# One merge over all units: projections two batches ahead, the network two units behind, maxima paced by VectorE

## The chip, the cores and the metric

The kernel runs on one core of one Trainium2 chip. The metric is the device time of one execution in microseconds, here the median of several runs. The engines of the core are TensorE (PE; its weight loads are shown as PEld), VectorE (DVE), ScalarE (ACT), GpSimd (POOL) and SyncE (SP), which issues the DMAs here. Each engine takes its instructions strictly in the order of its own queue, and waits on semaphores for the others.

## What is computed

The input x has 8 batches of 1024 tokens with 512 features, in float32. A layer norm without weights gives xn. The output is x plus causal attention of xn plus a gated network of xn, where the network's operands are first rounded to a 4-bit grid with one scale for each block of 16.

```python
def fp4_quant_dequant(x):
    xb = x.reshape(shape[:-1] + (shape[-1] // BLOCK, BLOCK))      # BLOCK = 16
    scale = jnp.maximum(jnp.max(jnp.abs(xb), axis=-1, keepdims=True) / 6.0, 1e-12)
    xn = xb / scale
    idx = jnp.searchsorted(_MID, jnp.abs(xn))
    return (_GRID[idx] * jnp.sign(xn) * scale).reshape(shape)

def fp4_linear(x, w):
    return jnp.einsum('bsk,nk->bsn', fp4_quant_dequant(x), fp4_quant_dequant(w))

# attention: 16 heads of 32, causal softmax, W_attn 512 x 1536, W_proj 512 x 512
qkv = xn @ W_attn + b_attn
att = softmax(where(causal, q @ k.T * 32 ** -0.5, -inf))
attn = (att @ v) @ W_proj + b_proj
# network: w_gate and w_up 1408 x 512, w_down 512 x 1408
ffn = fp4_linear(silu(fp4_linear(xn, w_gate)) * fp4_linear(xn, w_up), w_down)
out = x + attn + ffn
```

## The kernel before

**Tiles and units.** Tokens are cut into 64 tiles of 128 (eight to a batch, numbered n through all batches). Attention is cut into 64 units of two heads of one batch. So there are as many units as tiles, and the work of the kernel goes in steps of one unit and about one tile of everything else.

**The stages that a tile passes.** `load_tokens`, `normed` (layer norm on DVE, with a power on POOL) and `prepare` transpose a tile. After every second tile `project` makes q, k and v for the pair: six groups of 16 matmuls over W_attn pieces `wa`, loaded anew each time, two buffers deep. ACT evicts a group to `full` (one buffer; L443 for q and k, L486 for v), DVE splits q and k in a high and a low part for the fp32r matmuls (`high`, one buffer), and SP stores them to `qk_kept` in DRAM (L462), v to `v_kept`. The rounded tile `xq`, transposed, goes to `xq_kept` and comes back later as `xqT_in` for the network.

**The stages that a unit passes.** `load_half` and `load_values` bring q, k and v back from DRAM. `maxima` (L535 to L563) computes the scores once, 24 matmuls of up to 512 columns, and reduces each on DVE (L545) to the row maxima, which are transposed and sent through DRAM to `shT`. `weigh` subtracts them and computes the scores again in PSUM (L627 and L630), takes the exponential on ACT (L638), sums on POOL (L603), multiplies with v (L609), and stores `y` and the sums. `invert` makes their reciprocals.

**The network.** `network` goes through each tile in chunks of 512, 512 and 384 hidden columns: gate and up products (L768), silu on ACT, product and rounding on DVE (the class `Quantised`, L292 to L316), transposition (L323), down product into `acc` (L748). Its weights are rounded and transposed once by `weights_quantised`, in 34 pieces; the first `EARLY` pieces give two of their steps to POOL. `finish` loads `y` and the inverses of a tile (L840, L846), forms their product on DVE (L852, L853), does the output projection (L861), adds the network's part, and stores the result.

**What sets the order.** The order on every queue is fixed when the program is built, by a planner in the kernel. Each stage is a generator that yields (cost on PE, earliest time of its next step, number of PSUM banks that it needs). `merge` takes several such streams, keeps a planned clock, and advances the stream that has done the least share of its total, among those within `AHEAD_OF_OTHERS` of the last one; if no one can start, the planned clock moves. `Later` issues an action at a planned time. There are six banks, handed out by `Banks`. The costs that the planner assumes (`dve(0.65)`, `act(...)`) are written by hand.

**Before the change** there is one `merge` for each unit, over the streams weigh(n), maxima(n + 1), prepare and project of tile n + 10 (`AHEAD`), network of tile n - 8 (`LAG`) and finish of tile n - 10. It ends when every stream has ended. Ahead of unit 0 stand a merge of eight tiles' projections with 17 weight pieces, and one of two further tiles with the maxima of unit 0. In units 0 to 7, where no network can run yet, the other 17 weight pieces are rounded, and `prepare_late` reads x again, norms and rounds the tiles 0 to 7. Behind unit 63 come eight merges with one tile of network and one or two of finish each.

Of the kernel before, what the change touches and what calls it, by code (L numbers as in the profile page):

```python
# [19 lines left out]
P = 128  # L20
# [7 lines left out]
def kernel(  # L28
# [27 lines left out]

    nc = tc.nc
# [15 lines left out]
    AHEAD = 10  # L73
    LAG = 8
    SPREAD = 1.4
    HOP = 0.15
    TABLE = 1.3
    AHEAD_OF_OTHERS = 0.3
# [13 lines left out]
    dram = ctx.enter_context(tc.tile_pool(name="dram", bufs=4, space=DRAM))  # L92
# [48 lines left out]
    def act(columns, after=0.0, function="other"):  # L141
        if function == "other":
            function = table[0]
        switch = TABLE if function != table[0] else 0.0
        table[0] = function
        return on("act", 0.1 + 0.00095 * columns + switch, after)
# [31 lines left out]
    class Banks:  # L178
# [9 lines left out]
        def take(self):  # L188
            k = self.at.index(min(self.at))
            self.at[k] = float("inf")  # L190
            return k, self.tiles[k]
# [30 lines left out]
    def load_biases():  # L222
# [3 lines left out]
        wide = p1.tile([P, NC, P], F32, name="xqT")  # L226
# [16 lines left out]
    class Quantised:  # L243
# [38 lines left out]
        def operations(self, src, w, xs, helper):  # L282
# [6 lines left out]
            spreader, name, cost = (nc.gpsimd, "pool", 1.1) if helper else (nc.vector, "dve", 0.68)  # L289
# [6 lines left out]
            def powers():  # L296
# [7 lines left out]
                    0.65,  # L304
# [6 lines left out]
                (0.15, 0.55, "dve", scales),  # L311
                (cost, 0.0, name, lambda: spreader.tensor_tensor(blocks(xs), blocks(src), spread(inv), ALU.mult)),
                (0.9, 0.0, "dve", powers),
                (0.67, 0.0, "dve", lambda: nc.vector.tensor_tensor(xs, xs, step, ALU.add)),
                (0.67, 0.0, "dve", lambda: nc.vector.tensor_tensor(xs, xs, step, ALU.subtract)),
# [48 lines left out]
    def normed(tl):  # L364

        xt = tl.xt
        stats = p4.tile([P, 6], F32, name="stats")
        mv = p4.tile([P, 2], F32, name="mv")
        rstd = p4.tile([P, 1], F32, name="rstd")
        nc.vector.bn_stats(stats, xt)  # L370
        nc.vector.bn_aggr(mv, stats)
        nc.vector.tensor_scalar_add(rstd, mv[:, 1:2], EPS)
        nc.gpsimd.tensor_tensor(rstd, rstd, power, ALU.pow)
        yield 0.0, pool(0.6, dve(1.05)), 0
        nc.vector.tensor_scalar(xt, xt, mv[:, 0:1], rstd, ALU.subtract, ALU.mult)
        tl.ready = dve(0.6)
        if tl.n >= NT:
            tl.xs = Quantised(xt, D, p1.tile([P, CW], F32, name="xs"))

    def prepare(tl):  # L380
# [7 lines left out]
        if tl.n >= NT:  # L388
            yield from keep_quantised(tl, tl.xs)
# [7 lines left out]
    def prepare_late(tl):  # L397
        xt = p3.tile([P, D], F32, name="res")
        nc.sync.dma_start(out=xt, in_=x[tl.b, tl.t * P : (tl.t + 1) * P, :])
        tl.xt = xt  # L400
        yield 0.0, clock[0] + 4.0, 0
        yield from normed(tl)
        xq = Quantised(tl.xt, D, tl.xt, tl.ready)
        yield from keep_quantised(tl, xq)

    kept = []
# [6 lines left out]
    def keep_quantised(tl, xq):  # L413
        yield 0.0, xq.ready(), 1
        settle(kept)
        xqT = p1.tile([P, NC, P], F32, name="xqT")
        end = transposed(xqT, xq.done(), NC)
        tl.xq = dram.tile([P, NC, P], F32, name="xq_kept", bufs=AHEAD + LAG + 4)
        kept.append(Later(end - clock[0] + 0.5, lambda: nc.sync.dma_start(out=tl.xq, in_=xqT)))
        yield 0.45, 0.0, 0  # L420

    def project(batch, g, after):
        xnT = batch.xnT
        yield 0.0, after, 1
        for s in range(2):
            for f in range(0, NC, 2):
# [28 lines left out]
                def split(full=full, high=high, low=low):  # L455
                    nc.vector.tensor_copy(high, full)
                    nc.vector.tensor_tensor(low, full, high.bitcast(F32), ALU.subtract)
                    dve(1.1)
# [62 lines left out]
    def maxima(un):  # L521
# [4 lines left out]
        for t in range(NT):  # L526
            Q, i = t // QG, t % QG
            for r in range(HU):
                k = i * HU + r
                for h in range(Q + 1):  # L530
# [15 lines left out]
                    end = dve(0.08 + 0.00105 * n, end)  # L546
                    banks.back(bank, end)
                    yield cost, 0.0, 1
# [10 lines left out]
        yield 0.0, dve(1.1), 1, 0.3  # L559
# [23 lines left out]
    def weigh(un):  # L583
        f, r0 = un.u * HU // HPC, un.u * HU % HPC
        emptied = 0.0
        yield 0.0, un.ready, 2
        for Q in range(2):
# [5 lines left out]
            def summed(group):  # L593

                for r in range(HU):
# [4 lines left out]
                    else:  # L600
                        for pr, q0 in prs:
                            pool(0.1 + (W - q0) * 0.0024)
# [66 lines left out]
            added = free["pool"]  # L669
            yield 0.0, max(ready, emptied), 0  # L670
            yield weighted(), added, 1
# [16 lines left out]
            emptied = act(W)  # L688
            zs = p2.tile([P, W // 2], F32, name="zs")
            nc.scalar.copy(zs, z)  # L690
            end = act(W // 2, clock[0] + 0.65)
# [15 lines left out]
            yield 0.65, 0.0, 2  # L707


        def invert():  # L710
            flat = HU * S // P
            z = p2.tile([P, flat], F32, name="z")
            nc.sync.dma_start(out=z, in_=un.batch.sums[un.u].rearrange("q g (p e) -> (q g p) e", e=flat))
            inverses = un.batch.inverses[un.u].rearrange("q r (p e) -> (q r p) e", e=flat)
            Later(5.0, lambda: nc.vector.reciprocal(z, z))
            Later(8.0, lambda: nc.sync.dma_start(out=inverses, in_=z))


    def load(tl):
        tl.xqT = p3.tile([P, NC, P], F32, name="xqT_in")  # L720
        nc.sync.dma_start(out=tl.xqT, in_=tl.xq)
        tl.there = clock[0] + 4.0

    def network(tiles):
# [8 lines left out]
        def down(job):  # L733
# [12 lines left out]
            for j in range(job.w // P):  # L746
# [4 lines left out]
                if i == NI - 1:  # L751
# [4 lines left out]
                    tl.part = dram.tile([P, D], F32, name="part_kept", bufs=NT + 8)  # L756
# [6 lines left out]
        def product(job, wT):  # L763
            yield 0.0, job.tl.there, 1
# [19 lines left out]
        def hidden(job):  # L784
            nc.vector.tensor_tensor(job.hid, job.hid, job.g, ALU.mult)
            end = dve(0.65, max(job.gated, clock[0] + 1.72 * job.w / CW))
# [3 lines left out]
        def jobs():  # L790
            for tl, following in zip(tiles, tiles[1:] + [None]):
                if following is not None:
                    Later(4.0, lambda following=following: load(following))
# [33 lines left out]
    def finish(tl):  # L827
        t = tl.t

# [20 lines left out]
        part = load_part() if tl.part is not None else None  # L850
# [3 lines left out]
        yield 0.0, dve(1.4), 1, 1.0  # L854
        for half in range(2):
# [8 lines left out]
            if part is None:  # L864
                while tl.stored is None:
                    yield 0.0, clock[0] + 1.0, 0
                part = load_part()
                yield 0.0, clock[0] + 4.0, 0
            nc.vector.tensor_tensor(part[:, cols], po, part[:, cols], ALU.add)
            end = dve(0.42, clock[0] + 1.72)  # L870
            banks.back(k, end)
            yield 1.72, 0.0 if resident else clock[0] + 6.0, 1
        Later(end - clock[0] + 0.5, lambda: nc.sync.dma_start(out=out[tl.b, t * P : (t + 1) * P, :], in_=part))


    class Batch:
        def __init__(self):
# [4 lines left out]
            self.inverses = dram.tile([NU, 2, HU, W], F32, name="inv_kept")  # L882

# [4 lines left out]
    class Tile:  # L888
        def __init__(self, n):
            self.n, self.b, self.t = n, n // NT, n % NT  # L890
            self.part, self.stored, self.ready, self.there = None, None, 0.0, 0.0
# [6 lines left out]
    def merge(streams):  # L898

        live = [Stream(total, steps) for total, steps in ((t, s) for s, t in streams)]  # L900
        while live:
            least = min(s.share() for s in live)
            start = lambda s: max(s.ready, banks.when(s.banks))
            near = [s for s in live if s.share() - least < AHEAD_OF_OTHERS] or live
            now = [s for s in near if start(s) <= clock[0] + 0.05]
            if now:
                s = min(now, key=Stream.share)
# [9 lines left out]
    class Stream:  # L917
        def __init__(self, total, steps):
            self.total, self.steps = total, steps
            self.done, self.ready, self.banks = 0.0, 0.0, 0  # L920

        def share(self):
            return self.done / self.total

        def step(self):
            said = next(self.steps, None)
            if said is None:
                return False
            cost, self.ready, self.banks = said[:3]
            self.done += said[-1] if len(said) > 3 else cost  # L930
            passed(cost)
            return True

    def run(steps):
        merge([(steps, 1.0)])
# [21 lines left out]
    EARLY = PIECES // 2  # L957
    tiles = [Tile(n) for n in range(N)]
    units = [Unit(n) for n in range(N)]
    batches = []  # L960

# [7 lines left out]
    with tc.manual_schedule(  # L969
# [17 lines left out]
        head = itertools.chain(*[begin(n) for n in range(NT)])  # L987
        merge([(head, 10.7 * NT), (up_to(weights_steps, EARLY * 0.5, [0.0]), EARLY * 0.5)])
        for un in units:
            un.batch = None  # L990
        for n in range(3):
            units[n].batch = batches[0]
# [11 lines left out]
        merge([(itertools.chain(begin(NT), begin(NT + 1)), 22.0), (first_maxima(), 4.7)])  # L1004
        load_biases()
        late = [0.01]
        for n in range(N):
            if n == N - AHEAD + 1:
                for half in range(2):
                    wp = p2.tile([P, NC, 2 * P], F32, name="wa")  # L1010
                    nc.sync.dma_start(out=wp, in_=wp_in[:, :, half * 2 * P : (half + 1) * 2 * P])
                    resident.append(wp)
            streams = []
            while units[n].shT is None:
                passed(0.5)
            if n + 2 < N:
                units[n + 2].batch = batches[units[n + 2].b]

            def loads(n=n):
                if n + 1 < N:  # L1020
                    load_half(units[n + 1], 1)
                if n + 2 < N:
                    load_half(units[n + 2], 0)
                if n + 1 < N:
                    load_values(units[n + 1])

            Later(1.0, loads)
            if n + AHEAD < N:
# [62 lines left out]
```

## Time and profile before

| | us |
|---|---|
| three runs | 4860.23, 4861.45, 4874.52 |
| median | 4861.45 |
| the profiled execution, its own time | 4870.0 |
| the profiled execution, its span | 4868.3 |

| engine | busy us | share of the span | instructions |
|---|---|---|---|
| PE | 4445.5 | 91% | 18708 |
| PEld | 2643.2 | 54% | 18708 |
| DVE | 3326.0 | 68% | 6937 |
| ACT | 1459.5 | 30% | 2892 |
| POOL | 1847.5 | 38% | 2618 |

The mean granted clock of TensorE is 0.96. The span runs from the first to the last instruction. Busy times of matmuls overlap[...]. The profile's slices show the busy share of each engine in 40 equal parts of the span, in tenths; a line with L and a number names a line of the kernel, and an arrow "x <- y" in a list of waits says that x stood until y was done, with the total, the count and the longest one.

### The profile page before, as it was taken

What the parts mean: (1) busy time and instruction counts of PE and PEld (TensorE: products, weight loads), DVE (VectorE), ACT (ScalarE), POOL (GpSimd) and SP (SyncE); (2) the same over time, 40 slices, a digit from 0 to 9 for tenths busy, and PEclk for the clock granted to TensorE, in tenths of its full rate; (3) what the DMA queues carried; (4) which work ended last, traced back from release to release, by engine and by line L of the source; (5) the groups of instructions that cost most, each with busy time, mean ns of one, the idle gap of its engine ahead of it and who ended that gap; (6) DMA issues with size and microseconds to landing.
All of it is one profiled execution on the core that took longest, in us unless ns stands there. A gap on an engine that the chain in (4) does not pass through costs nothing.

```text
span 4868.3 us, 59460 instructions
## 1 busy us (share of the span) xinstructions
PE 4445.5 (91%) x18708; PEld 2643.2 (54%) x18708; DVE 3326.0 (68%) x6937; ACT 1459.5 (30%) x2892; POOL 1847.5 (38%) x2618
## 2 busy tenths in 40 slices
PE   6577779999999999999999999999999999999998
PEld 5444445555555555555555555555555555555544
DVE  5677776666776766667767676777766667766544
ACT  1122223333333333333333333333333333333200
POOL 2144444334343433443334334443333344444300
PEclk8778889999999999999999999999999999999999
DMA  5644443355444544554544455445444543332221
GB/s 173 179 111 119 112 119 103 106 148 145 127 138 136 140 121 137 148 142 124 140 137 136 123 150 142 133 133 141 136 121 136 146 133 103 84 90 75 68 63 54
DMA packets 609146, 605.36 MB, mean 124 GB/s; under 512 B 133824, under 2 KB 464064, under 8 KB 608832
## 3 DMA queue, kind: packets, MB, share of 16 engines
q1 hardware_dynamic: 608832, 601.57, 44.3%
q8 instruction: 149, 2.44, 0.2%
q14 instruction: 165, 1.35, 0.1%
HBM read 431.50 MB, written 169.87 MB: 124 GB/s over the span
## 4 chain that ended last, share of the span: by engine, by line
PE 53%; DVE 25%; DMA 11%; POOL 3%; SPq 3%; issue 2%; ACT 1%; ACTq 0%; DVEq 0%; POOLq 0%
PE bank L768 16%; PE acc L748 9%; DVE neg L545 4%; PE bank L432 4%; PE y L609 4%; PE bank L627 3%; PE bank L535 3%; PE bank L630 3%; PE bank L861 3%; PE bank L476 3%; DMA qs<-qk_kept 3%; PE bank L323 2%; DMA z<-sums_kept 2%; POOL sum L603 2%; DMA ks<-qk_kept 2%
## 5 line engine op out<-in xcount | busy, mean ns | idle before, releaser
L603 POOL TENSOR_TENSOR sum<-sum,pr 128x512 f32<-128x512 f32 (+3 forms) x1024 | 988.8, 976 | 749.3 <-ACT pr L638 714.2
L638 ACT ACTIVATE pr<-bank 128x512 f32<-128x512 f32 (+3 forms) x1536 | 679.5, 491 | 1070.2 <-PE bank L630 859.7
L545 DVE TENSOR_REDUCE neg<-bank 128x1 f32<-128x512 f32 (+3 forms) x1536 | 840.6, 555 | 173.6 <-PE bank L535 138.0
L543 DVE TENSOR_TENSOR bank<-bank,mask 128x128 f32<-128x128 f32 x1024 | 299.0, 292 | 655.6 <-PE bank L535 655.0
L535 PE MATMUL bank<-ks,qs 128*128 128x512 f32 (+3 forms) x1536 | 659.8, 472 | 85.8 <-DVE neg L545 46.1
L627 PE MATMUL bank<-shT,pick 128*128 128x512 f32 (+3 forms) x1536 | 653.4, 433 | 56.4 <-DVE neg L545 56.0
L768 PE MATMUL bank<-wgT,xqT_in 128*128 128x512 f32 (+1 forms) x1536 | 688.6, 578 | 3.8 <-ACT hqT L324 0.7
L768 PE MATMUL bank<-wuT,xqT_in 128*128 128x512 f32 (+1 forms) x1536 | 680.3, 574 | 2.2 <-ACT pr L638 2.1
L644 POOL TENSOR_SCALAR_AFFINE_SELECT pr<-pr 128x128 f32<-128x128 f32 x1024 | 344.8, 352 | 878.6 <-ACT pr L638 872.7
L748 PE MATMUL acc<-wdT,hqT 128*128 128x512 f32 x1408 | 670.7, 596 | 1.3 <-ACT hqT L324 1.3
L630 PE MATMUL bank<-qs,ks 128*128 128x512 f32 (+3 forms) x1536 | 531.4, 354 | 0.0
L598 POOL TENSOR_TENSOR sum<-pr 128x512 f32<-128x512 f32 x256 | 350.0, 1391 | 359.4 <-ACT pr L638 359.4
L432 PE MATMUL bank<-xnT,wa 128*128 128x256 f32 x2048 | 475.9, 387 | 3.2 <-DMA wa<-in_L_attn_W_attn_dram 1.4
L535 PEld LDWEIGHTS bank<-ks,qs 128*128 128x128 f32 x1536 | 281.6, 194 | 337.8 <-issue 123.7
L432 PEld LDWEIGHTS bank<-xnT,wa 128*128 128x128 f32 x2048 | 394.6, 195 | 81.4 <-issue 20.8
L609 PE MATMUL y<-pr,vs 128*32 128x512 f32 (+3 forms) x3072 | 391.2, 523 | 42.4 <-POOL pr L644 39.1
L627 PEld LDWEIGHTS bank<-shT,pick 128*128 128x128 f32 x1536 | 301.9, 197 | 228.0 <-DVE neg L545 90.1
L768 PEld LDWEIGHTS bank<-wgT,xqT_in 128*128 128x128 f32 x1536 | 273.2, 192 | 250.5 <-issue 191.8
L768 PEld LDWEIGHTS bank<-wuT,xqT_in 128*128 128x128 f32 x1536 | 285.0, 195 | 213.1 <-issue 160.6
L748 PEld LDWEIGHTS acc<-wdT,hqT 128*128 128x128 f32 x1408 | 255.5, 190 | 218.0 <-issue 202.4
L630 PEld LDWEIGHTS bank<-qs,ks 128*128 128x128 f32 x1536 | 301.7, 196 | 85.2 <-issue 52.0
L443 ACT ACTIVATE full<-bank,bqk 128x256 f32<-128x256 f32 x256 | 107.6, 472 | 630.5 <-PE bank L432 263.5
(98 smaller groups left out, 4833.5 us busy)
## 6 DMA issues: line engine op xcount, KB each, us to landing
wa<-in_L_attn_W_attn_dram SPq DMA_DIRECT2D x192, 512.0 KB
qs<-qk_kept SPq DMA_DIRECT2D x512, 128.0 KB
ks<-qk_kept SPq DMA_DIRECT2D x512, 128.0 KB
wp<-in_L_attn_W_proj_dram SPq DMA_DIRECT2D x93, 512.0 KB
qk_kept<-high SPq DMA_DIRECT2D x128, 256.0 KB
qk_kept<-full SPq DMA_DIRECT2D x128, 256.0 KB
y_kept<-yu SPq DMA_DIRECT2D x256, 128.0 KB
yT<-y_kept SPq DMA_DIRECT2D x128, 256.0 KB
```

Of the source, the lines that this page charges most:

```text
L432: nc.tensor.matmul(pq[:, j, :], lhsT=wa[:, c, j * P : (j + 1) * P], rhs=xnT[:, c, :], start=(c == 0), stop=(c == NC - 1),)
L535: nc.tensor.matmul(sc[:, :n], lhsT=un.qs[Q][:, r, i * P : (i + 1) * P], rhs=un.ks[h][:, r, :n], start=True, stop=True,)
L545: nc.vector.tensor_reduce(neg[:, Q + h, k : k + 1], sc[:, :n], AX.X, ALU.max, negate=True)
L598: nc.gpsimd.tensor_tensor(sums[r], prs[0][0], prs[1][0], ALU.add)
L603: nc.gpsimd.tensor_tensor(sums[r][:, q0:], sums[r][:, q0:], pr[:, q0:], ALU.add)
L609: nc.tensor.matmul(y[row : row + HD, q0:], lhsT=un.vs[h][:, jj, r * HD : (r + 1) * HD], rhs=pr[:, q0:], start=(j < 2), stop=(j >= last - 1 ...
L627: nc.tensor.matmul(w[:, q0:], lhsT=pick[:, Q * HU + r, :], rhs=un.shT[:, q0:], start=True, stop=False)
L630: nc.tensor.matmul(w[:, q0:], lhsT=un.ks[h][:, r, jj * P : (jj + 1) * P], rhs=un.qs[Q][:, r, q0:], start=False, stop=True,)
L638: nc.scalar.activation(pr[:, q0:], w[:, q0:], AF.Exp)
L644: nc.gpsimd.affine_select(out=pr[:, q0 : q0 + P], in_=pr[:, q0 : q0 + P], compare_op=ALU.is_ge, fill=0.0, base=0, pattern=[[1, P]], channe ...
L748: nc.tensor.matmul(tl.acc, lhsT=job.hqT[:, j, :], rhs=wdT[:, i, :], start=(i == 0), stop=(i == NI - 1))
L768: nc.tensor.matmul(job.g, lhsT=job.tl.xqT[:, c, :], rhs=wT[:, c, job.i0 : job.i0 + job.w], start=(c == 0), stop=(c == NC - 1),)
```

## The change

The merges of the single units give way to one merge over everything. A stream is now a row of parts; each part has a place on an axis that counts units (`begin`, `length`), and the merge advances the stream that is furthest back on this axis, among those within 0.6. Streams that could have started 0.4 us ago (`SURE`) go first.

- Projections run 16 tiles ahead of the units (formerly 10): the start projects two batches, in two merges, with 14 weight pieces beside each, and with the maxima of unit 0 in the second. Six pieces are left for the units 0 and 1.
- The network runs two units behind (formerly 8). `finish` of tile n begins at unit n + 10, once all units of its batch are done.
- `prepare_late` is gone. The normed tile is kept in DRAM (`xn_kept`), and `quantised` brings it back, rounds and transposes it one unit ahead of the network.
- `maxima` yields `free["dve"] - QUEUE` as the earliest time of its next step: DVE's planned queue has to be under 2 us. It begins 0.3 units earlier.
- The planner's costs are changed, mostly raised (DVE and POOL steps, `HOP` from 0.15 to 0.2); `finish` adds its halves by `Later`, and the reciprocals are planned 14 us after their load instead of 5.

The core of the diff:

```diff
-    AHEAD = 10
-    LAG = 8
+    AHEAD = 2 * NT
+    LAG = 2
+    LAST = NT + 2
+    SOONER = 0.3
+    QUEUE = 2.0
+    SURE = 0.4
...
-    HOP = 0.15
+    HOP = 0.2
     TABLE = 1.3
-    AHEAD_OF_OTHERS = 0.3
+    AHEAD_OF_OTHERS = 0.6
...
-            spreader, name, cost = (nc.gpsimd, "pool", 1.1) if helper else (nc.vector, "dve", 0.68)
+            spreader, name, cost = (nc.gpsimd, "pool", 1.35) if helper else (nc.vector, "dve", 0.7)
...
-                (0.9, 0.0, "dve", powers),
+                (1.14, 0.0, "dve", powers),
...
-        if tl.n >= NT:
-            tl.xs = Quantised(xt, D, p1.tile([P, CW], F32, name="xs"))
+        tl.xn = dram.tile([P, D], F32, name="xn_kept", bufs=AHEAD + LAG + 4)
+        tl.kept = Later(tl.ready - clock[0] + 0.5, lambda: nc.sync.dma_start(out=tl.xn, in_=xt))
...
+    def quantised(tl):
+
+        tl.kept.now()
+        xs = p1.tile([P, CW], F32, name="xs")
+        nc.sync.dma_start(out=xs, in_=tl.xn)
+        yield 0.0, clock[0] + 4.0, 0
+        xq = Quantised(xs, D, xs)
+        yield 0.0, xq.ready(), 1
+        xqT = p3.tile([P, NC, P], F32, name="xqT")
+        tl.there = transposed(xqT, xq.done(), NC)
+        tl.xqT = xqT
+        yield 0.45, 0.0, 0
...
-                    end = dve(0.08 + 0.00105 * n, end)
+                    end = dve(0.16 + 0.00103 * n, end)
                     banks.back(bank, end)
-                    yield cost, 0.0, 1
+                    yield cost, free["dve"] - QUEUE, 1
...
     def finish(tl):
         t = tl.t
+        while tl.batch.units_done < NU or tl.stored is None:
+            yield 0.0, clock[0] + 1.0, 0
...
-            least = min(s.share() for s in live)
+            least = min(s.at for s in live)
...
-    EARLY = PIECES // 2
+    EARLY = PIECES - 6
...
+        merge(
+            [
+                Stream([(prepared(NT, AHEAD), 10.8 * NT, 0.0, 1.0)]),
+                Stream([(up_to(weights_steps, part, late), part, 0.0, 1.0)]),
+                Stream([(first_maxima(), 6.0, 0.3, 0.7)]),
+            ]
+        )
...
+        def networks():
+            yield weights_steps, (PIECES - EARLY) * 0.5, 0.0, LAG
+            for n in range(N):
+                yield up_to(net, TILE), TILE, n + LAG, 1.0
+
+        def preparations():
+            for n in range(AHEAD, N, QT):
+                yield prepared(n, n + QT), 10.8 * QT, n - AHEAD, QT
+            yield last_weights(), 1.0, N - AHEAD + 1, 0.0
+
+        merge(
+            [
+                Stream((weigh(un), 17.5, un.n, 1.0) for un in units),
+                Stream((maxima(un), 6.0, un.n - 1 - SOONER, 1.0) for un in units[1:]),
+                Stream(networks()),
+                Stream((quantised(tl), 0.45, tl.n + LAG - 1, 0.5) for tl in tiles),
+                Stream(preparations()),
+                Stream((finish(tl), 4.5, tl.n + LAST, 1.0) for tl in tiles),
+            ]
+        )
```

## The prediction

> **What bounds the kernel now.** I began with the page's slices. They split the span in two: a start in which TensorE (PE) is busy about seven tenths at a lowered clock, and a long remainder at nine tenths.
>
> ```profile
> PE   6577779999999999999999999999999999999998
> ...
> PEclk8778889999999999999999999999999999999999
> ```
>
> Next I looked for the stage borders in the rows of single lines. The first attention weight (L627) is at 267.6 us, the first network product (L768) at 763.4, the last value projection (L476) at 3991.5, the last L627 at 4556.9. Busy time between these borders (columns: sum, then PE, PEld, DVE, ACT, POOL, granted clock, DMA share, GB/s):
>
> ```profile
> 0.00:268.00 268.00, 162.28 (x662) 129.72 (x663) 154.96 (x340) 41.12 (x84) 49.77 (x61) 0.80 0.58 173
> 268.00:763.00 495.00, 370.01 (x1618) 226.34 (x1617) 375.75 (x765) 138.79 (x309) 230.96 (x320) 0.82 0.42 114
> 763.00:3996.00 3233.00, 3085.89 (x13307) 1844.86 (x13307) 2262.79 (x4715) 1056.61 (x2071) 1278.20 (x1839) 0.99 0.48 134
> 3996.00:4565.00 569.00, 551.10 (x2321) 297.54 (x2320) 382.73 (x804) 196.94 (x382) 278.43 (x390) 0.99 0.34 89
> 4565.00:4868.30 303.30, 276.23 (x807) 144.75 (x805) 149.76 (x314) 26.04 (x47) 10.13 (x8) 0.99 0.20 61
> ```
>
> So the kernel has five stages. Start: 268 us for ten projected tiles and half the weight pieces. Units 0 to 7 without the network: 495 us, 61.9 each. Units 8 to 53 with everything: 3233 us, 70.3 each. Units 54 to 63 without projections: 569 us, 56.9 each. Tail, eight networks and ten output projections: 303 us. In the third to fifth stage PE sets the time. In the first two it doesn't: nothing of the network can run there.
>
> Last, the waits. In the start PE stands behind weight pieces that VectorE (DVE) and GpSimd haven't finished:
>
> ```profile
> PE bank L323 <- POOL hid L316: 41.7, 9, 7.7
> ```
>
> In a steady stretch (1114 to 2097 us, 14 units) PE's own waits are few, mostly for the maxima's reductions; all five rows are shown:
>
> ```profile
> PE bank L627 <- DVE neg L545: 16.2, 7, 2.9
> PE bank L861 <- DVE neg L545: 9.4, 6, 1.6
> PE bank L535 <- DVE neg L545: 5.7, 11, 2.0
> PE bank L561 <- DVE stat L557: 4.2, 7, 0.6
> PE bank L677 <- ACT full L443: 3.3, 3, 2.1
> ```
>
> They sum to 38.8 us, 2.8 us a unit. Better pacing can win no more than this in the steady stage. For 3996 to 4565 the same view sums to 17.6 us, 1.8 a unit.
>
> **What the Trainium skill says.** "Perfetto Trace Analysis", Identifying the Most-Contended Engine, warns that matmul busy time doesn't tell how near PE is to its limit. I agree here: 512-column fp32 records start every 0.43 us and are booked as 0.59, so I use waits and stage lengths, not the 91%. "TensorE: Matmul & The Clock Gate", What's actually happening, says recent activity opens the clock and idling closes it. The trace agrees: 0.80 and 0.82 in the two starved stages, 0.99 after. "DMA: Bandwidth & Descriptors", Anatomy of one DMA, fits about 2.0 us plus bytes/436e3 (on GpSimd's path), an estimate of 2.6 us for 256 KB. Here, on SP's queue, the last store and load of 256 KB took 2.01 and 2.56 us, and I use these.
>
> **The change, part by part.** PE's matmuls are the same in both kernels, only reordered. So I price the stages.
>
> Start. Sixteen tiles, eight pairs, are now projected before unit 0, with 28 weight pieces instead of 17. Pairs began at 13, 64, 104, 150 and 204 us: 47 us a pair. In the pair at 104, the projections alone took 26 us, paced by evicting (L443), splitting, and storing `full` before it is reused. Some 18 us of PE gaps followed, at weight pieces, about 4.3 us for each of the 4.25 pieces per pair. With 3.5 pieces a pair: 26 + 15 + 1 for one more 256 KB store per tile, beside the others, gives 42. Start: 13 + 8 x 42 + 20 (the last pair to the first L627, as before) = 369, say 370 us. The bounds are 36 a pair, since the planner's raised DVE and POOL costs call pieces later, and 47: 320 to 410. Unit 0's maxima lie beside it.
>
> Units 0 and 1 without the network. Before, 46 to 50 us where no projection fell in the unit, about 79 where a whole pair did; a pair is now spread over two units. Each has three pieces rather than two, all on DVE (one costs 5.9 us from the rows L292 to L316), but no second layer norm. I take 52 each, 105 together (90 to 130).
>
> Steady units. Of the 62 others, 46 have projections (units 2 to 47) and 16 don't. Work per unit is equal: `xn_kept` stores and loads replace `xq_kept` ones one for one, and the fp32 to fp32r switches, counted in the two PE orders, are 46.0 and 47.5 a unit. PE's work by columns alternated 56 and 76 us between units, and is now 66 and 66. The maxima end 21 to 33 us of PE work ahead of their unit, formerly 12 to 18, which should end the waits on `stat` (L561). I let half of the waits go: 70.3 - 1.4 = 68.9 and 56.9 - 0.9 = 56.0. The bounds: all of them gone, or 3 us more each. Sum: 46 x 68.9 + 16 x 56.0 = 3169 + 896 = 4065.
>
> Tail. Behind unit 63, PE's order has two networks with part of the ten output projections, some 66 us of columns, 73 with the tail's present tenth of idling. After the last down product, **eight output projections stand alone**, one behind another, because `finish` starts tile n at unit n + 10 and the network ends at 66. Each waits for its predecessor: `yT0` is one buffer, and its load queues on SP until PE has read it. One costs 2.9 us of issuing (the two loads L840 and four L846 issued from 4848.05 to 4851.0), about 2.0 landing of the last, 1.5 for two DVE steps, 3.7 for 16 records of L861, 0.2 of hops: 10.2. Eight are 82. Tail 155 (140 to 175).
>
> VectorE gets eight layer norms less and the SP queue eight reloads of `x`: beside other work, nothing. The later `reciprocal` of the sums delays only `finish`, ten units behind: nothing. The wait of the maxima for DVE's queue is in the planner, not on the chip; it has no instruction.
>
> Sum: 370 + 105 + 4065 + 155 = 4695, against a span of 4868.3 and 4870.0 of the profiled run. That run is 8.5 over the median of 4861.45. 4695 + 1.7 - 8.5 = 4688, so **4690**.
>
> **Rivals.** *Steady stage unmoved.* For it: every freed wait there is small, and the chain names PE anyway. 46 x 70.3 + 16 x 56.9 = 4144, so 79 more: about 4767.
>
> *The start keeps 47 us a pair*, steady unmoved. For it: one write of `full` or `high` must land before the next eviction, and its buffers don't change; 32 waits on that store cost ACT 208 us. Against: fewer pieces per pair. 13 + 8 x 47 + 20 = 409: about 4806.
>
> *Slower: bursts of maxima.* The pacing lets maxima pass whenever DVE's planned queue is under 2 us. In PE's order, 31% of the maxima of the steady units now follow another at once, formerly 23%, and the DVE time that they ask for in 4 us of PE work passes 1.20 of that time in one place of ten (formerly 0.94). On the chip, the quantising steps queued between them hold the banks, and PE, in order, stands at the next L627 or network product. Three us more a unit than now give 4767 + 62 x 3 = 4953. It decides from 94/62 = 1.5 us a unit. Against: the planner's DVE prices are now nearer the durations of the rows (1.14 for two steps of 0.64 + 0.46), so it calls results later.
>
> *It doesn't do what it says.* "Without barriers" holds until unit 63; the eight lonely projections are a new drain, in the sum already.
>
> **How the numbers follow.** Forecast case (half to all steady waits gone): 0.50, its own range 4610 to 4740. Unmoved: 0.22. Old start: 0.13. Bursts: 0.15, of which 0.12 is slower by over 0.3% and 0.03 within it; 0.01 of the third case is within it too. A measurement of this kernel can tell about 0.3%, 15 us. Faster 0.84, same 0.04, slower 0.12. The range 4600 to 4830 holds the first case but for a little, the second, and most of the third: about 0.82.
>
> **What would show it.** The first L657 (was L627) near 370 us; the first L785 (was L768) near 475 rather than 763. Clock in the start still about 0.8. Steady units of 68 to 70 us, with less PE waiting on neg (L545, in the changed kernel L548). The last L763 some 80 us before the end, then eight equal groups of L878, PE busy about a third. I am wrong if the start takes over 410 us, if steady units take over 72, or if the tail is much under 140.

## The result, and the profile after

The changed kernel takes 4802.93 us (median of four runs, 4794.69 to 4807.12), the kernel before, measured beside it, 4864.16: a ratio of 0.9869, 95% interval 0.9848 to 0.9890. It is 61 us faster. The forecast was 4690, so the direction was right and the size was not: a third of it came. The profiled execution took 4794.69 us; its span of 4792.7 is to be compared with the 4695 of the prediction's sum. The median missed by 113 us and this span by 98: the profiled execution lies 8 us under its median, and the prediction had taken off 8.5 us because that of the kernel before lay above.

The slices of the page first: the seven tenths at a lowered clock are over after four slices, formerly six to seven, and a new drop to four tenths stands in the last slice.

```profile
PE   6566999999999999999999999999999899999994
...
PEclk8788999999999999999999999999999999999997
```

The stages again, by the same rows of the changed kernel's trace: first L657 (was L627), third unit, last projection, last L639 (was L609), last L763 (was L748), end. Columns as before: sum, PE, PEld, DVE, ACT, POOL, clock, DMA share, GB/s.

```profile
0.00:379.00 379.00, 234.73 (x984) 191.15 (x984) 197.39 (x418) 60.92 (x126) 76.14 (x89) 0.81 0.60 183
379.00:493.00 114.00, 87.13 (x436) 59.23 (x436) 83.13 (x189) 36.46 (x79) 52.18 (x79) 0.86 0.49 131
493.00:3662.00 3169.00, 3005.39 (x13198) 1847.39 (x13188) 2284.89 (x4699) 1047.58 (x2069) 1364.35 (x1838) 0.99 0.48 132
3662.00:4613.00 951.00, 877.49 (x3775) 496.94 (x3775) 708.52 (x1458) 321.37 (x623) 446.98 (x624) 0.96 0.33 84
4613.00:4691.50 78.50, 69.13 (x206) 36.50 (x201) 41.31 (x89) 7.47 (x15) 2.55 (x2) 0.96 0.20 59
4691.50:4792.70 101.20, 43.62 (x128) 33.48 (x127) 17.18 (x31) 0.00 (x0) 0.00 (x0) 0.75 0.32 96
```

Dividing gives 68.9 us for each of 46 units (3169) and 59.4 for each of 16 (951). The last row has a clock of 0.75 and PE busy for 43%. Against the prediction's sum:

| stage | predicted | measured | missed |
|---|---|---|---|
| start | 370 | 379 | 9 |
| units 0 and 1 | 105 | 114 | 9 |
| units 2 to 47 | 46 x 68.9 | 46 x 68.9 | 0 |
| units 48 to 63 | 16 x 56.0 | 16 x 59.4 | 55 |
| network behind unit 63 | 73 | 78.5 | 5.5 |
| lonely output projections | 82 | 101.2 | 19 |

These sum to the 98 us that the span is longer than the forecast. PE's waits in units 2 to 47 of the changed kernel, in full but for four rows under 5 us:

```profile
PE bank L331 <- DVE xs L324: 106.5, 42, 4.6
PE bank L657 <- ACT full L444: 21.3, 18, 2.8
PE bank L538 <- DMA ks<-qk_kept: 17.0, 15, 1.9
PE bank L657 <- DVE neg L548: 5.8, 22, 0.7
```

The waits on the reductions of the maxima (neg), of which I let half go, are nearly gone: 5.8 us in 46 units, formerly 31.3 in 14. A wait that wasn't in the list of the kernel before took their place: the transposition of the rounded tile `xs`.

There is a second difference inside these 46 units. `finish` starts in unit 10 in both kernels: the first output projection (L878) is at 1054.5 us, and unit 10 begins at 1016.

```profile
L878 PE MATMUL bank<-wp,yT x624: 379/379/484, 1054.5 to 3712.4; 128*128 128x256 f32 x156
```

So of the 46 units eight have no output projection, 2 to 9; of the 46 that I took the 70.3 us from, only two had none. Units 2 to 9 take 65.3 us each, and units 10 to 47, which have everything, 69.6. The difference of 4.3 is near the 3.7 us of a projection's sixteen records. The like units before are 10 to 53, at 70.1 us. The rows of units 2 to 9 and 10 to 47 in the changed kernel, then of 10 to 53 in the kernel before:

```profile
493.00:1016.00 523.00, 496.15 (x2178) 300.25 (x2168) 375.34 (x789) 181.13 (x359) 234.86 (x319) 0.98 0.41 112
1016.00:3662.00 2646.00, 2509.25 (x11023) 1547.14 (x11021) 1909.56 (x3910) 866.45 (x1711) 1129.49 (x1519) 0.99 0.49 136
```

```profile
911.00:3996.00 3085.00, 2951.45 (x12760) 1766.85 (x12759) 2168.53 (x4518) 1009.46 (x1981) 1222.06 (x1759) 0.99 0.49 136
```

Among like units the merge gains only 0.5 us each, and PE's idle time in them even grew, from 3.0 to 3.6 us. So the 68.9 us was right for other reasons than mine. In the units 48 to 63 the same row is nearly twice as heavy per unit, and almost alone:

```profile
PE bank L331 <- DVE xs L324: 65.2, 15, 8.4
PE bank L538 <- DMA qs<-qk_kept: 6.7, 2, 5.9
```

The timeline shows one of these waits: PE, in its fixed order, has finished a maxima's product (L538) at 4276.9, and stands 8.4 us at the transposition (L331), with the next weights (L657) behind it in its order. Between two steps of xs (L320 and L305) VectorE did all the remaining ones of another piece (`hid`). Columns are start, duration, engine, line, operation, tiles.

```profile
4276.06 0.80 PE L538 MATMUL bank<-ks,qs 128*128 128x512 f32 x1
4285.27 1.09 PE L331 MATMUL bank<-ident,xs 128*128 128x128 f32 x4 [8.41 <-DVE xs L324]
```

```profile
4275.15 0.68 DVE L320 TENSOR_TENSOR xs<-xs,inv 128x512 f32<-128x512 f32 x1
4275.75 0.68 DVE L802 TENSOR_TENSOR hid<-hid,bank 128x512 f32<-128x512 f32 x1
4276.35 0.82 DVE L320 TENSOR_TENSOR hid<-hid,inv 128x512 f32<-128x512 f32 x1
...
4281.45 0.69 DVE L324 TENSOR_TENSOR hid<-hid,scale 128x512 f32<-128x512 f32 x1
4282.06 0.42 DVE L305 TENSOR_SCALAR step<-xs 128x512 int32<-128x512 int32 x1
```

### The profile page after: what moved, and what is told of

Read it like the earlier page. It is cut to its first block, busy times and chain, and to the rows that moved or that the text cites. A ratio compares the mean times of both kernels' runs of the same rounds, so it can differ in the third digit from the quotient of the medians.

```text
span 4792.7 us, 59517 instructions
## 1 busy us (share of the span) xinstructions
PE 4317.5 (90%) x18708; PEld 2664.7 (56%) x18708; DVE 3332.4 (70%) x6883; ACT 1473.8 (31%) x2910; POOL 1942.2 (41%) x2632
## 4 chain that ended last, share of the span: by engine, by line
PE 52%; DVE 25%; DMA 15%; SPq 3%; issue 3%; ACT 1%; POOL 0%; DVEq 0%; ACTq 0%; POOLq 0%
PE bank L785 16%; PE acc L763 6%; PE bank L878 4%; PE bank L538 4%; PE bank L657 4%; PE bank L433 4%; PE y L639 4%; PE bank L660 4%; DMA ks<-qk_kept 3%; DMA qk_kept<-full 3%; DMA inv_y<-inv_kept 3%; DMA qs<-qk_kept 3%; PE bank L331 2%; DVE step L308 2%; PE bank L477 2%
## 5 line engine op out<-in xcount | busy, mean ns | idle before, releaser
L633 POOL TENSOR_TENSOR sum<-sum,pr 128x512 f32<-128x512 f32 (+3 forms) x1024 | 1000.1, 987 | 428.8 <-ACT pr L668 392.9
L674 POOL TENSOR_SCALAR_AFFINE_SELECT pr<-pr 128x128 f32<-128x128 f32 x1024 | 388.7, 393 | 1225.9 <-ACT pr L668 1217.8
L538 PE MATMUL bank<-ks,qs 128*128 128x512 f32 (+3 forms) x1536 | 703.9, 505 | 53.1 <-DMA ks<-qk_kept 17.7
L785 PE MATMUL bank<-wuT,xqT 128*128 128x512 f32 (+1 forms) x1536 | 682.3, 571 | 0.0
L763 PE MATMUL acc<-wdT,hqT 128*128 128x512 f32 x1408 | 677.3, 602 | 1.4 <-ACT hqT L332 1.4
L785 PE MATMUL bank<-wgT,xqT 128*128 128x512 f32 (+1 forms) x1536 | 660.5, 563 | 0.0
L657 PE MATMUL bank<-shT,pick 128*128 128x512 f32 (+3 forms) x1536 | 605.7, 402 | 31.0 <-ACT full L444 25.2
L628 POOL TENSOR_TENSOR sum<-pr 128x512 f32<-128x512 f32 x256 | 362.4, 1440 | 608.2 <-ACT pr L668 608.2
L538 PEld LDWEIGHTS bank<-ks,qs 128*128 128x128 f32 x1536 | 284.4, 191 | 328.3 <-issue 195.3
L657 PEld LDWEIGHTS bank<-shT,pick 128*128 128x128 f32 x1536 | 294.1, 191 | 221.1 <-issue 106.2
L785 PEld LDWEIGHTS bank<-wgT,xqT 128*128 128x128 f32 x1536 | 279.9, 191 | 233.7 <-issue 180.6
L785 PEld LDWEIGHTS bank<-wuT,xqT 128*128 128x128 f32 x1536 | 283.5, 195 | 205.6 <-issue 161.2
L763 PEld LDWEIGHTS acc<-wdT,hqT 128*128 128x128 f32 x1408 | 257.9, 191 | 225.0 <-issue 208.8
L639 PE MATMUL y<-pr,vs 128*32 128x512 f32 (+3 forms) x3072 | 361.7, 518 | 0.0
```

Of the source, the lines that this page charges most:

```text
L538: nc.tensor.matmul(sc[:, :n], lhsT=un.qs[Q][:, r, i * P : (i + 1) * P], rhs=un.ks[h][:, r, :n], start=True, stop=True,)
L628: nc.gpsimd.tensor_tensor(sums[r], prs[0][0], prs[1][0], ALU.add)
L633: nc.gpsimd.tensor_tensor(sums[r][:, q0:], sums[r][:, q0:], pr[:, q0:], ALU.add)
L639: nc.tensor.matmul(y[row : row + HD, q0:], lhsT=un.vs[h][:, jj, r * HD : (r + 1) * HD], rhs=pr[:, q0:], start=(j < 2), stop=(j >= last - 1 ...
L657: nc.tensor.matmul(w[:, q0:], lhsT=pick[:, Q * HU + r, :], rhs=un.shT[:, q0:], start=True, stop=False)
L674: nc.gpsimd.affine_select(out=pr[:, q0 : q0 + P], in_=pr[:, q0 : q0 + P], compare_op=ALU.is_ge, fill=0.0, base=0, pattern=[[1, P]], channe ...
```

## The experiments

My theory after the result: the missed time lies in two places, the rounding of x in units that had none before, and the chain of lonely output projections; the rest of the change did as forecast. Rivals: these late units are bound by attention or the clock itself; pacing, lag or costs took back what other parts gave. Ratios are to the kernel before, measured beside each, with 95% intervals. Stage times are from one profile each, by the same rows as above; the profiled executions lie up to some 12 us off their medians.

**Rounding left out late (noround).**

```diff
-        xq = Quantised(xs, D, xs)
-        yield 0.0, xq.ready(), 1
+        if tl.n < 3 * N // 4:
+            xq = Quantised(xs, D, xs)
+            yield 0.0, xq.ready(), 1
+            xs = xq.done()
...
-        tl.there = transposed(xqT, xq.done(), NC)
+        tl.there = transposed(xqT, xs, NC)
```

> The changed kernel, with the rounding of x left out for the tiles 48 to 63: their normed tiles go to the network unrounded. Theory (the rounding of x, which before was done beside the projections and so not in the last ten units, now runs on VectorE in the units 48 to 63, and TensorE stands at its transposition, 62 us of waits on xs in 3800 to 4565 us): the units 48 to 63 fall from 59.4 us to 55 to 57 each, the run by 40 to 70 us, to about 4750. Rival (these units are bound by the attention itself, or by the clock of 0.96 there): less than 15 us, about 4795.

Ratio 0.9663 (0.9645 to 0.9681), about 100 us faster than the changed kernel, more than the 40 to 70 of the theory. Units 48 to 63 fall from 59.4 to 53.8 us; the other stages stay within 16 us. The stage's row of this kernel:

```profile
3681.00:4541.00 860.00, 855.65 (x3775) 488.10 (x3774) 644.02 (x1308) 322.90 (x623) 449.08 (x624) 1.00 0.36 93
```

PE has the same 3775 instructions, is busy for all but 4 us, and its clock is 1.00 rather than 0.96. So neither the attention nor the clock held these units at 59.4 us, and the low clock went with the waits. The rounding costs these units 5.7 us each. Its steps keep DVE busy for 4.0 us a unit ((708.5 - 644.0) / 16), and PE's wait on xs was 4.1 (65.2 / 16).

**The rounding sooner, its transposition later (lead).**

```diff
-        yield 0.0, xq.ready(), 1
+        yield 0.0, xq.ready() + 8.0, 1
...
-                Stream((quantised(tl), 0.45, tl.n + LAG - 1, 0.5) for tl in tiles),
+                Stream((quantised(tl), 0.45, tl.n + LAG - 1.5, 0.5) for tl in tiles),
```

> The changed kernel, with the rounding of x begun half a unit sooner and its transposition planned 8 us later than the planner thinks it ready. Theory (TensorE waits at that transposition because the planner calls it before VectorE, running behind its plan, has got through): the waits on xs, 106 us in units 2 to 47 and about 75 us in units 48 to 63, mostly go, and the run falls by 100 to 150 us, to about 4680. Rival (VectorE is the bound in these stretches, and the wait only moves to the maxima or to the transposition of hid): less than 30 us, about 4785.

Ratio 0.9676 (0.9660 to 0.9693), some 94 us faster than the changed kernel. All the rounding is done, VectorE is as busy, and the wait is nearly gone, but another has come. Waits of PE in units 2 to 47:

```profile
PE bank L538 <- DMA qs<-qk_kept: 73.6, 24, 7.6
PE bank L706 <- POOL sum L633: 26.3, 24, 1.3
PE bank L331 <- DVE xs L324: 9.9, 22, 0.5
```

So the transposition was indeed called too early for the rounding that it waits on; which of the two edits did more isn't separated. Units 48 to 63 take 57.4 us, which brings back 32 of the 55 us missed there. The rest of the gain, some 56 us, is in units 2 to 47. The rival has a part of it: some wait moved, though to the load of q, which the planner takes for landed as soon as it is issued.

**Two buffers for yT0 (finish2).**

```diff
-            yT = p1.tile([P, NC, P], F32, name=f"yT{part}")
+            yT = (p1 if part else p2).tile([P, NC, P], F32, name=f"yT{part}")
```

> The changed kernel, with two buffers for yT0 in the output projection, so that the loads of the next tile need not wait until TensorE has read the last one. Theory (the eight output projections at the end are one chain of loads, two VectorE steps and matmuls, 13.1 us each): the loads, 2.4 us of issuing and 4.2 us of landing, then lie beside the matmuls of 5.5 us, about 8 us each, 41 us less in all, about 4762. Rival (the chain is set by the landing of the many small packets of inv, and by the SP queue, which the next tile's loads also need): 10 us less or nothing, about 4795.

Ratio 0.9770 (0.9753 to 0.9788). That is 1.0 points, some 48 us, better than the changed kernel. In the profile the last stage falls from 101.2 to 64.8 us, 8.1 a projection, and nothing else moves by more than 6 us: the theory. One step of the chain in the changed kernel shows the terms:

```profile
4707.93 0.92 SPq L857 DMA_DIRECT2D yT<-y_kept  x2
4709.01 1.80 SPq L863 DMA_DIRECT2D inv_y<-inv_kept  x4
...
4711.83 0.69 DVE L869 TENSOR_TENSOR yT<-yT,yT 128x512 f32<-128x512 f32 x1 [3.40 <-DMA yT<-y_kept]
4714.99 0.69 DVE L870 TENSOR_TENSOR yT<-yT,inv_y 128x512 f32<-128x512 f32 x1 [2.46 <-DMA inv_y<-inv_kept]
4715.73 5.54 PE L878 MATMUL bank<-wa,yT 128*128 128x256 f32 x16 [7.84 <-DVE yT L870]
...
4721.30 0.92 SPq L857 DMA_DIRECT2D yT<-y_kept  x2
```

The chain that ended last has the load between them:

```profile
4710.38 4.48 DMA inv_y<-inv_kept
```

From the first load to the next tile's are 13.4 us. The last `inv` is issued at 4710.4 and is there at 4714.9, 4.5 us later (I had 2.0), and the sixteen records take 5.5 us (I had 3.7) in a stage whose clock is 0.75. Issuing (2.5 us, I had 2.9) and the DVE step that follows the landing (0.7; I had 1.5 for two) were cheaper than I thought.

**No pacing (nopace).**

```diff
-                    yield cost, free["dve"] - QUEUE, 1
+                    yield cost, 0.0, 1
```

> The changed kernel, with the maxima not paced by VectorE's planned queue. Theory (pacing took away the waits of TensorE for the maxima's reductions, 35 us in 14 units before and 6 us in 46 units after): they come back, 1 to 2 us a unit, the run is 60 to 120 us longer, about 4890. Rival (the waits went because projections are spread and maxima begin sooner, or the wait on xs took their place): within 20 us of 4803.

Ratio 1.0527 (1.0511 to 1.0542): not 60 to 120 us but some 320 slower than the changed kernel, and the stages from unit 0 to 63 are longer (units 8 to 47 74.4 us, 48 to 63 67.1). The bursts that I gave 15% as a rival are real, and pacing is what holds them off: in PE's order of units 2 to 47, 47% of the maxima's records follow another directly, in series of up to 16. In the changed kernel it is 31%, in series of up to three. PE stands for the reductions again, though at the maxima's own products (L538), and so do its weight loads:

```profile
PE bank L538 <- DVE neg L548: 68.2, 76, 2.1
```

```profile
PEld bank L538 <- DVE neg L548: 104.1, 109, 2.6
```

The units 2 to 47 are 4.5 us longer each. PE's idle time takes 1.9 of this; its busy time takes the other 2.6, at a clock of 0.96 rather than 0.99.

**The network eight units behind (lag8),** `LAG = 8` in the changed kernel.

> The changed kernel with the network eight units behind again (LAG 8), all else as changed. Theory (the gain is that six network tiles lie in the units 2 to 7, where they cost about 8 us each, instead of behind unit 63, where they cost 37; eight lonely output projections, 101 us less the 10 us of before, take half of it back): 6 x 29 - 92 = 82 us longer, about 4885. Rival (it is the projections two batches ahead and the pacing that gain, and the lag is neutral, since what it wins it gives back at the end): within 25 us of 4803.

Ratio 0.9849 (0.9833 to 0.9866): no different from the changed kernel. The rival held. Six networks less behind unit 63 save 154 us (333.5 of tail against 179.7). But units 2 to 7 without the network take 44.6 us in the new merge, 21 less than the 65.7 of the changed kernel, so a network tile there costs 21 us and not the 8 of my theory: 6 x 21 + 14 in units 0 and 1 = 141 us. (With this lag the planner also spreads the last six weight pieces over eight units.) The network's place is neutral while `yT0` is one buffer: of the 179.7 us of tail 101 are the lonely projections, and here they are 20. A lag of 8 with two buffers wasn't run.

**The old costs (oldcosts),** the changed kernel with `HOP = 0.15` and the old numbers in `dve(...)`, `pool(...)`, `act(...)` and the steps of `Quantised`.

> The changed kernel with the planner's costs and HOP of the kernel before. Theory (raised costs make the planner call DVE and POOL results later, so TensorE stands less in its fixed order): waits on xs and hid grow, the start grows by 20 to 40 us, the run by 60 to 150 us, to about 4900. Rival (TensorE is slower on the chip than in the plan anyway, which hides it): within 20 us.

Ratio 1.0166 (1.0150 to 1.0181), 3.0% or 146 us slower than the changed kernel. Units 8 to 47 take 72.9 us; the start grows by 6 us only. The wait on xs is more than twice the 106.5 us of the changed kernel:

```profile
PE bank L331 <- DVE xs L324: 230.8, 43, 10.6
```

**Pacing, costs, and both in the kernel before (bpace, bcosts, bboth).** The edits are those of the diff, alone.

> The kernel before, with the pacing of the maxima alone. Theory (leaving the pacing out of the changed kernel cost 5.4%, so pacing is worth as much by itself, up to the 2.8 us a unit of waits on the maxima's reductions in the steady units): 60 to 150 us shorter, about 4770. Rival (before, the shares within a unit's merge already spread the maxima over the unit, and pacing only matters where that is gone): within 25 us of the kernel before.

> The kernel before with the planner's costs and HOP of the changed kernel, nothing else. Theory (the costs are worth 3.0% in the changed kernel because they make the planner call results later, and this holds in any merge): 40 to 120 us shorter than before. Rival (before has no rounding close to its use in the steady units, where the low costs did harm; so nothing is there to be won): within 25 us of before.

> The kernel before with the changed kernel's costs and the pacing of the maxima. Theory (pacing alone made it 1.2% slower because it goes by a queue of VectorE that the old costs understate; with right costs it helps): 50 to 130 us shorter than before. Rival (with a barrier at each unit's end, maxima that are held back end late and lengthen the unit, whatever the costs): longer than before by 20 to 80 us.

Ratios 1.0119 (1.0103 to 1.0136), 1.0230 (1.0197 to 1.0262) and 1.0334 (1.0309 to 1.0359). All three are slower than the kernel before. The three theories of a gain fell, and so did the rivals of bpace and bcosts, which said no change; bboth is what its rival said, and more. The steady units 8 to 47 take 71.2, 71.9 and 72.7 us, formerly 70.3. In bpace most of this is one wait: on `stat` (L561), for the end of the maxima, PE stands 42.7 us in these units, formerly 14.2. Held-back maxima end late there. For bcosts the cause stays open. Parts that the changed kernel can't do without do harm in the old one.

**The lead among the streams (near03, nopace03).** To see on what pacing depends, `AHEAD_OF_OTHERS` was put back to 0.3, with and without pacing.

> The changed kernel with AHEAD_OF_OTHERS at 0.3 and the pacing kept. Theory (with pacing the wider lead is a gain, since more streams are at hand when one waits): 30 to 100 us longer than 4803. Rival (the lead is neutral once the maxima are paced): within 20 us.

> The changed kernel without the pacing of the maxima (as in nopace) and with AHEAD_OF_OTHERS at 0.3, as before the change. Theory (unpaced maxima do harm because the stream may run 0.6 units ahead, and then fills VectorE's queue and the banks): most of nopace's 330 us come back, about 4880 or less. Rival (the lead is not it; in the one merge a stream with no wait of its own is always ready and goes first): over 5050.

| in the changed kernel | paced | not paced |
|---|---|---|
| streams up to 0.6 units ahead | 0.9869 | 1.0527 |
| up to 0.3 units ahead | 1.0338 (1.0318 to 1.0357) | 1.0193 (1.0164 to 1.0222) |

Neither expectation had this size: near03 loses 230 us, and nopace03 gets half of nopace's loss back. Of the four cells only the one with both settings is faster than the kernel before. With a lead of 0.3, pacing costs 1.4 points here, as it cost 1.2 in the kernel before. In near03 PE stands at xs again (221.6 us between 700 and 3400 us, 91.1 in the changed kernel). That a held-back stream, being the last, then holds all others back is how I read it; it wasn't measured by itself.

**Two changes of the start (nohelper, wide).** `helper=False` for all weight pieces; and `full` in two buffers.

> The changed kernel, with the weight pieces rounded on VectorE alone, none of their steps on GpSimd. Theory (in the start TensorE stands 76 us at the transposition of pieces whose last step is GpSimd's; 2 steps of 1.2 us and their hops become 2 of 0.7): the start falls from 379 us to 340 to 360, the run by 20 to 40 us. Rival (it is VectorE's chain and its place in the order that is late, and VectorE gets 40 us more work): no change or up to 20 us more.

> The changed kernel with two buffers for full, into which ScalarE evicts q, k and v. Theory (the projections of a pair take 26 us because the eviction waits until the store of full has landed, 121 us of waits in the start): the start falls by 20 to 60 us, the run by as much. Rival (high has one buffer too, and its store is issued just ahead, so VectorE's split takes over the wait): under 15 us.

nohelper: 0.9859 (0.9835 to 0.9884), nothing. The start is 378 us, and PE still stands 59.1 us at the pieces, now for VectorE, where it stood 75.8 for GpSimd. So it isn't GpSimd's slower steps alone that set the start. wide: 0.9751 (0.9728 to 0.9774), 1.2% faster than the changed kernel. That is the size that I expected, by luck, for it isn't where I looked. The start falls by 8 us only; the waits on the store turn up in part before other groups. The rest is in the units: 2 to 47 take 32 us less in all, and PE's 21.3 us behind ACT's eviction (`L657 <- ACT full`) are gone from the list.

**The waits together (best2, best3).** best2 has lead, finish2, and in `maxima`

```diff
+            if i == 0:
+                yield 0.0, un.landed[Q], 1
```

where `landed` is 6 us behind the load of a half. best3 adds wide, with one buffer for `zs`.

> The changed kernel with the rounding sooner and its transposition later (as in lead), two buffers for yT0 (as in finish2), and maxima that wait in the plan until their half of q and k, loaded 6 us ago, has landed. Theory (three separate waits: xs 85 us, yT0 37 us, and qs, on which lead's TensorE stood 74 us in units 2 to 47): 85 + 37 + 30 to 70 less, about 4630. Rival (the wait on qs moves on to the weights' start on shT, as the maxima end later): 85 + 37 less and no more, about 4680.

> The changed kernel with the edits of lead, finish2 and wide and the landing wait of best2 together; the small tile zs has one buffer instead of two to make room. Theory (the waits on xs, yT0, qs and on full are separate terms, so wide's 1.2% comes on top of best2): ratio to the kernel before 0.942 to 0.948. Rival (they lie in the same gaps, and TensorE or VectorE now binds): 0.952 to 0.958, as best2.

best2: 0.9568 (0.9552 to 0.9584), 3.0 points or some 146 us under the changed kernel, between the theory's 152 to 192 and the rival's 122. Units 48 to 63 take 56.2 us and the last stage 64.1. The wait on `qs` is gone, but units 8 to 47 still take 69.4. The wait moved on, as the rival said, though not to shT in these units but to GpSimd's work:

```profile
PE y L642 <- POOL pr L677: 41.4, 18, 3.1
PE bank L709 <- POOL sum L636: 35.7, 37, 1.4
```

best3: 0.9546 (0.9530 to 0.9561), no clear step beyond best2, as its rival said: wide's 1.2% didn't come on top. The list of best2 shows a reason: the wait that wide takes away, of the weights behind ACT's eviction, isn't in it any more. That the smaller `zs` took a gain back isn't excluded, but ACT's waits before `zs` are 65.1 us in best2 and 66.4 in best3. best3 beats both kernels; it is 4.5% faster than the one before.

Not run by themselves were the projections two batches ahead, the earlier start of the maxima (`SOONER`), `SURE`, and the changes in `finish` and `invert`.

## Why the prediction was wrong

**The step that failed** is "Work per unit is equal: `xn_kept` stores and loads replace `xq_kept` ones one for one." That holds for the whole run, not for each stage. Before, tile n + 10 was rounded with its projection, so units 54 to 63 had no rounding of x; their 56.9 us, from which I took the 56.0, are a price without it. With the network two units behind, tiles 47 to 62 are rounded and transposed in units 48 to 63, and these take 59.4. This is 55 of the 98 us. noround shows the price, 5.7 us a unit, and without it the stage would have taken 53.8, under my 56.0.

More than half of this price is standing and not work. With the same rounding, called in better order, the stage takes 57.4 us a unit (lead), and 56.2 when the landing of q is planned too (best2), which is my figure within 0.2. So what I put at nothing was PE's wait for a rounding that is called close to its use: 65.2 us in these units. DVE's column shows the work that came: 38 us busy a unit in units 54 to 63 before (382.7 in 10 units), 44 in the changed kernel's units 48 to 63.

**The second term** is the lonely projections, seen rightly in PE's order and undersized: 10.2 us each instead of about 13. I took the landing of the last `inv` at 2.0 us, about that of a store of 256 KB, while it is one of four broadcasts of 64 KB behind two loads; and I took matmul times of a busy stage for a stage that idles. I had quoted that idling closes the clock, and used it in no price. The tail of 180 us is above my bound of 175.

**The start** took 9 us more than the sum, by two errors that nearly cancel. The pairs came at 46 us, not 42. (The old ones, which I put at 47, were 47.7 apart from 13 to 204 us.) The last pair took 44 us to the first L657, where I had put 42 + 20. The 208 us of ACT's waits on the store, which I gave for the rival, are those of the whole run; in the old start they are 76. Neither more eviction buffers nor taking GpSimd out moved the start by more than some 8 us. What sets it stays open; PE's waits there are at weight pieces still (75.8 us). Units 0 and 1 were 9 us over the sum too, within my bounds; their cause wasn't looked for.

**The steady units** were right to 0.1 us by luck. The maxima's waits fell by far more than half, the early call of xs put 2.3 us a unit in their place, and PE's idle time grew. What brought the mean down is for the most part that eight of the 46 units have no output projection: "work per unit is equal" fails here too, in the kernel's favour, and I counted these projections at the end without taking them off here. Why like units are 0.5 us shorter with more idle time stays open. That a planner which issues rounding near its use makes PE wait for it in its fixed order is the wait that I should have looked for: `quantised` adds one, and I had named only the planner's own.

**The rivals.** Bursts do decide, but the pacing prevents them: nopace is slower than the kernel before, and lies beyond my 4953. "The start keeps 47 us a pair" (4806) came nearest in time, by luck: its pairs are nearly right, and the steady units, like for like, hardly moved, but its start of 409 us is 30 too long, and its units 48 to 63 are too short. The network's lag, which I took for a main source of gain, gives none (lag8).

## What to carry to other kernels

When work is moved from one stage to another, price the stages that receive it and those that lose it separately: a stage's old time is a price only for the same contents. In a kernel with a fixed order per engine, look for each step that now comes closer to its use, and ask who stands behind it. Settings of a scheduler are not additive: pacing and costs did harm in the old kernel and were needed in the new one, so undoing one part tells what it is worth beside the others, not by itself. And when a mean agrees with a forecast, look whether all its members have the same contents.

## What was not expected of the hardware

The granted clock went with small waits: with 74 us of gaps in 951 the stage of units 48 to 63 ran at 0.96, and in noround, with 4 in 860, at 1.00. The lonely projections ran at 0.75; the first of them, right behind the network, took 3.6 us for its sixteen matmul records, the seven others 5.3 to 6.1. The last of four broadcast loads of 64 KB landed 4.0 to 4.8 us after its issue, though the DMA engines were busy for a third of the time.
